# Output projection of a graph attention layer: chunk pairs per block, sums listed at the end of a step, another block order in the second pass

## The chip, the cores and the metric

The kernel runs on one core of a Trainium2 chip. The metric is the device time of one execution in microseconds; of several runs the median is taken. One further execution is recorded by the hardware profiler, and all the rows below come from it.

## What is computed

384 nodes with 1024 features go through one attention layer with an edge mask, in fp32:

```python
h = relu(layernorm(x))                                   # 384 x 1024
q, k, v = h @ wq.T + bq, h @ wk.T + bk, h @ wv.T + bv
q2, k2, v2 = q @ wiq.T + biq, k @ wik.T + bik, v @ wiv.T + biv   # each as 16 heads of 64
scores = einsum('hnd,hmd->hnm', q2, k2) / 8 + mask       # mask: softplus weight per edge type, -inf elsewhere
out = einsum('hnm,hmd->hnd', softmax(scores), v2)        # 384 x 1024
result = x + out @ wo.T + bo
```

The change is in the last line, out @ wo.T, and in how it is mixed with the heads.

## The kernel before

**Splitting.** Each fp32 product is made of three fp32r matmuls: high by high, high by low, low by high (mm3, L373 to L376). So every weight chunk (128 rows, 1024 columns) is split into a high and a low plane after it is loaded: the high one by ACT (L81) or VectorE (L79), the low one by VectorE or GpSimd (both L86). Loads are issued on SP's queue (L69), into four buffers.

**Phases.** First come the layer norm and the projections v, q, iv and k, while VectorE and GpSimd build the mask. Then one loop over steps (L825) does the attention and, in its gaps, what is left of the projections. This loop is where the change lies.

**The step loop.** Step i handles one tile i of the scores: head i // 3, row block i % 3, 48 tiles in all. What one tile passes through is spread over steps:
- S(i), step i: two score matmuls into one of two PSUM banks of tag "s" (L711).
- ttr(i), step i+1: VectorE adds the mask and takes the row's extreme, which reads that bank (L717).
- exp(i), step i+2: ACT (L721).
- recip(i), step i+3: VectorE (L734), and for i % 3 == 0 a scaling of it (L736); for the others GpSimd normalises the tile (L738).
- for i % 3 == 0: high(i) on ACT (L744, step i+3), low(i) on VectorE (L748, step i+4), and a transposing DMA on SP's queue (L752).
- the other two tiles of a head are transposed on TensorE (L758) some steps later, together with the matmuls of the attention by v2 (L773); a step with these is longer. ACT (L766) and VectorE (L767) take the transposed tiles from PSUM one step later, ACT (L793) and VectorE (L794) the head's output, and ACT (L798) and GpSimd (L799) split it into the planes of ao.

All of it is recorded in the order in which the Python code runs, and each engine works off its own list in that order. So where a line of code stands decides what is queued behind it.

**The filling.** In each step fill() is called before and after S(i) and gives TensorE some more matmuls from a generator. First fill_qk() gives the projections of q2 and k2 for the later heads; a finished projection is taken out by qk_done (L384, L385), which also issues the copies ks<-nat (L590). Then fill_o() gives the output projection.

**The output projection.** There are six output blocks a = 0 to 5 (a row block of 128 by 512 columns, list OT, L655) and eight chunks k of wo. Block (a,k) is three matmuls of 512 columns (omm, L650). Only three banks of tag "g" are free for sums, so there are two passes. The first takes chunks 0 to 3 (KH = 4) of each a; the sum is then added to the residual in SBUF by VectorE, ysum (L660 to L664), and the bank is free for another a. The second takes chunks 4 to 6 of a = 0 to 4, on three g banks and two s banks; the last part after the loop takes chunk 7, adds and stores. A block waits for its chunk's preparation (wready, two steps after it) and for the heads that it needs (6k + 18).

**When a ysum is listed.** A finished a is put on the list ysums. flush_y(1) inside fill_o() records one ysum just ahead of each bank("g") (L681, L697), that is, when a later a asks for the bank.

**When a chunk is prepared.** Chunks 0 and 1 are prepared while the q2 and k2 chunks are. Chunks 2 to 7 are prepared at the end of the steps listed in WSTEPS (L852), by wo_prep (L639): chunk 2 by VectorE (high) and GpSimd (low), 3, 4 and 6 by ACT and GpSimd, 5 and 7 by ACT and VectorE. wo_prep(k) also issues the load of chunk k+3, so that of chunk 2 issues the load of chunk 5.

Of the kernel before, what the change touches and what calls it, by code (L numbers as in the profile page):

```python
# [26 lines left out]
def gnn_kernel(ctx: ExitStack, tc: tile.TileContext, x, edges, erows, etw, wq, wk, wv, wiq, wik, wiv, wo,  # L27
# [20 lines left out]
    def bank(tag):  # L48
        return psum.tile([128, 512], F32, tag=tag, name=tag, bufs={"g": 3, "a": 1}.get(tag, 2))
# [545 lines left out]
    def run_tasks():  # L595
        while tasks:
            tasks.pop(0)()
# [31 lines left out]

    DT = (0,)  # L630
    PRE, RATE, RATE_O, RATE_E = 84, 7.9, 8, 8
    WSTEPS = (37, 40, 42, 44, 47, 51)
    PAR, OPOOL, ODVE = 1, (2, 3, 4, 6), (2,)

    otile = {}
# [1 line left out]
    KH = 4  # L637

    def wo_prep(k):  # L639

        dst = None
        if k == 4:
            otile[0] = gtile("g3").rearrange("p a k n -> p (a k n)")
        if 4 <= k < 7:
            g, b = otile[0], (k - 4) * 2048
            dst = (g[:, b:b + 1024], g[:, b + 1024:b + 2048])
        split(WO + k, nc.gpsimd if k in OPOOL else None, dst, k in ODVE)
        load(WO + k + 3)

    def omm(t, h, k, c=(0, 512)):  # L650
        hi, lo = (a[:, h * 512 + c[0]:h * 512 + c[1]] for a in whl[WO + k])
        mm3(oacc[t, h][:, c[0]:c[1]], ao[:, 0, k, t * 128:(t + 1) * 128], ao[:, 1, k, t * 128:(t + 1) * 128],
            hi, lo, k in (0, KH), k in (KH - 1, KT - 1))
# [6 lines left out]
    def ysum(a, c=(0, 512)):  # L660
        t, h = OT[a]
        y = xb[t][:, h * 512 + c[0]:h * 512 + c[1]]
        nc.vector.tensor_tensor(y, oacc[t, h][:, c[0]:c[1]], y, OP.add)  # L663
        return y  # L664
# [3 lines left out]
    def flush_y(n=6):  # L668
        for _ in range(min(n, len(ysums))):
            ysum(ysums.pop(0))  # L670

    def fill_o():


        first = [(0, 0), (0, 1), (1, 0), (1, 1), (2, 0), (2, 1)]
        first += [(a, k) for k in (2, 3) for a in range(3)] + [(a, k) for a in range(3, 6) for k in range(KH)]
        for a, k in first:
            while now[0] < wready[k] or now[0] < 6 * k + OREADY:
                yield 0
            if k == 0:  # L680
                flush_y(1)  # L681
                oacc[OT[a]] = bank("g")
            omm(*OT[a], k)
            if k == KH - 1:
                ysums.append(a)
            yield 4
        bank_step = (0, 0, 0, 49, 50)
        todo = [(a, k) for k in range(KH, 7) for a in range(5)]
        while todo:
            ready = [q for q in todo if now[0] >= max(6 * q[1] + OREADY, wready[q[1]], bank_step[q[0]])]  # L690
            if not ready:
                yield 0
                continue
            a, k = ready[0]
            todo.remove(ready[0])
            if k == KH:
                flush_y(1)  # L697
                oacc[OT[a]] = bank("gggss"[a])
            omm(*OT[a], k)
            yield 4  # L700
# [4 lines left out]
    def do_S(i):  # L705
        h, t = divmod(i, 3)
        p, o = divmod(h, 2)
        qs, ks = stacks["q", p], stacks["k", p]
        ps = st_ps[i] = bank("s")
        for s in range(2):  # L710
            nc.tensor.matmul(ps[:, :N], qs[:, o, t * 128:(t + 1) * 128], ks[:, o, s, :], start=(s == 0), stop=(s == 1))  # L711

    def do_ttr(i):
        t = i % 3
        e = es[i] = work.tile([128, N], F32, tag="e", name="e", bufs=EB)
        s = sts[i] = work.tile([128, 4], F32, tag="s", name="s", bufs=12)
        nc.vector.tensor_tensor_reduce(e, st_ps.pop(i)[:, :N], ma[:, t, :], -0.125, 3.0e38, OP.add, OP.min, s[:, 0:1])  # L717

    def do_exp(i):
        s = sts[i]  # L720
        nc.scalar.activation(es[i], es[i], AF.Exp, bias=s[:, 0:1], scale=-1.0, accum_out=s[:, 1:2])  # L721
# [10 lines left out]
    def do_norm(i):  # L732
        s = sts[i]
        nc.vector.reciprocal(s[:, 2:3], s[:, 1:2])  # L734
        if i % 3 in DT:
            nc.vector.tensor_scalar(s[:, 2:3], s[:, 2:3], PSC, None, op0=OP.mult)  # L736
        else:
            nc.gpsimd.tensor_tensor(es[i], es[i], s[:, 2:3].to_broadcast([128, N]), OP.mult)  # L738
# [3 lines left out]
    def do_high(i):  # L742
        planes[i] = plv[i // 3 % 3]
        nc.scalar.activation(planes[i][:, 0, :], es[i], AF.Copy, scale=sts[i][:, 2:3])  # L744

    def do_low(i):
        pl = planes[i]
        nc.vector.scalar_tensor_tensor(pl[:, 1, :], es.pop(i), sts[i][:, 2:3], pl[:, 0, :], op0=OP.mult, op1=OP.subtract)  # L748

    def do_turn(i):  # L750
        h, t = divmod(i, 3)
        nc.sync.dma_start_transpose(ptv[h % 3][:, :, t * 128:(t + 1) * 128],  # L752
                                    planes.pop(i).rearrange("p a n -> p (a n)"))
# [7 lines left out]
    def do_pt(i):  # L761
        h, t = divmod(i, 3)
        pt = ptv[h % 3]
        hi, lo = (pt[:, s * 3:s * 3 + 3, t * 128:(t + 1) * 128] for s in range(2))
        pv = tps.pop(i)[:, :N].rearrange("p (k n) -> p k n", k=3)
        nc.scalar.activation(hi, pv, AF.Copy, scale=PSC)  # L766
        nc.vector.scalar_tensor_tensor(lo, pv, PSC, hi, op0=OP.mult, op1=OP.subtract)  # L767
# [9 lines left out]
    def turns_and_av(tiles, heads):  # L777
        a, b = ([g(x) for x in xs] for g, xs in ((turn_mm, tiles), (av_mm, heads)))
        a, b = (itertools.chain(*x) for x in (a, b))
        end = object()  # L780
        while True:
            x, y = next(a, end), next(b, end)
            if x is end and y is end:
                return

    def do_ao(h):
        p, o = divmod(h, 2)
        if o == 0:
            aof[p] = work.tile([128, N], F32, tag="aof", name="aof")
        tmp = work.tile([128, N], F32, tag="aot", name="aot", bufs=1)  # L790
        ps = avs.pop(h)
        m, l = slice(o * 64, o * 64 + 64), slice(64 - o * 64, 128 - o * 64)
        nc.scalar.activation(tmp[m, :], ps[l, :N], AF.Identity, scale=down[l], bias=bc[m, 40 + p:41 + p])  # L793
        nc.vector.scalar_tensor_tensor(aof[p][m, :], ps[m, :N], down[m], tmp[m, :], op0=OP.mult, op1=OP.add)  # L794

    def do_aos(h):
        p = h // 2
        nc.scalar.activation(ao[:, 0, p, :], aof[p], AF.Copy)  # L798
        nc.gpsimd.tensor_tensor(ao[:, 1, p, :], aof[p], ao[:, 0, p, :].bitcast(F32), OP.subtract)  # L799

    gens = [fill_qk(), fill_o()]
    credit = [0.0]

    def fill(n):
        credit[0] += n
        while credit[0] > 0 and gens:
            try:
                c = next(gens[0])
            except StopIteration:
                gens.pop(0)  # L810
                continue
            if c == 0:
                credit[0] = 0.0
                return
            credit[0] -= c
# [9 lines left out]
    for i in range(S + 11):  # L825
        now[0] = i
        r = RATE if len(gens) == 2 else RATE_O if i < S else RATE_E
        fill(r / 2)
        if i < S:
            do_S(i)  # L830
        fill(r / 2)
        if 0 <= i - 1 < S:
            do_ttr(i - 1)
        if 0 <= i - 4 < S and (i - 4) % 3 in DT:
            do_low(i - 4)
        if 0 <= i - 2 < S:
            do_exp(i - 2)
        if 0 <= i - 3 < S:
            do_norm(i - 3)
            if (i - 3) % 3 in DT:  # L840
                do_high(i - 3)
        turns_and_av(t_at.get(i, []), [a_at[i]] if i in a_at else [])
        for x in t_at.get(i - 1, []):
            do_pt(x)
        if i - 1 in a_at:
            do_ao(a_at[i - 1])
        if a_at.get(i - 2, 0) % 2:
            do_aos(a_at[i - 2])
        run_tasks()
        if 0 <= i - 4 < S and (i - 4) % 3 in DT:  # L850
            do_turn(i - 4)
        if i in WSTEPS:  # L852
            wo_prep(wp)
            wready[wp] = i + 2
            wp += 1
    while gens:
        now[0] = 999
        fill(999)
# [55 lines left out]
```

## Time and profile before

| | us |
|---|---|
| median of 3 runs | 296.02 |
| the runs | 296.02, 294.78, 296.08 |
| the profiled execution | 294.56 |
| its span, from the first instruction to the last | 292.8 |
| TensorE busy in the span | 284.7 |
| VectorE busy | 208.2 |
| ACT busy | 159.7 |
| GpSimd busy | 154.8 |

The engines are called PE (TensorE), PEld (its weight loads), DVE (VectorE), ACT, POOL (GpSimd) and SP (the engine that issues DMAs) in the rows. A row of the timeline gives the start and the duration in us, the engine, the line of code, the operation, output<-inputs with their shapes, and in brackets how long the engine stood idle before it and what released it. Several like instructions in a row are merged (x2), with the time of all. A table by stages gives for each stretch the busy time of PE, PEld, DVE, ACT and POOL with the number of instructions, the granted clock of TensorE, the mean share of the DMA engines and what they moved in GB/s. A row of the waits names the engine and the instruction that waited, then the one waited for, the us in total, how often, and the longest. The chain of waits is followed back from the last instruction; "issue" in it is time for which the profile shows no wait.

### The profile page before, as it was taken

The numbers are of one execution on the slowest core, as the hardware profiler recorded it, in microseconds if no ns is written. First come the engines' busy times: TensorE is split into PE (matmuls) and PEld (weight loads), VectorE is DVE, ScalarE is ACT, GpSimd is POOL, SyncE is SP. The second block draws the span as 40 slices with busy tenths as digits, with TensorE's granted clock in tenths as the row PEclk, the third lists the DMA queues.
The fourth block names the chain that finished last, engine by engine and source line by source line (L and its number), as shares of the span: only waits on it lengthen the run. The fifth ranks groups of instructions, "written<-read, shape, count | busy, mean of one in ns | idle before, by whom it ended". The sixth has DMA issues, their size and how long they took to land. (4 is left out here: it accounts for less than half of the span.)

```text
span 292.8 us, 4859 instructions
## 1 busy us (share of the span) xinstructions
PE 284.7 (97%) x1610; PEld 267.4 (91%) x1610; DVE 208.2 (71%) x509; ACT 159.7 (55%) x291; POOL 154.8 (53%) x153
## 2 busy tenths in 40 slices
PE   6999999999999999999999999999999999989995
PEld 5999999999988889999999999999999998868874
DVE  3858996667665452999966768878786876788623
ACT  3894543244331222343643778787878788766510
POOL 3765576437775787992004256262627268636210
PEclk9999999999999999999999999999999999999999
DMA  7799857973463342278438879879797969901105
GB/s 268 248 321 404 292 209 254 323 242 112 143 189 122 121 146 72 72 224 296 154 86 227 241 208 211 212 166 227 166 234 147 254 133 234 230 2 27 27 3 215
DMA packets 33305, 54.60 MB, mean 187 GB/s; under 512 B 17408, under 2 KB 20992, under 8 KB 33280
## 3 DMA queue, kind: packets, MB, share of 16 engines
q1 hardware_dynamic: 30896, 51.90, 61.4%
q0 software_dynamic: 2064, 1.80, 2.2%
q10 hardware_dynamic: 320, 0.59, 0.8%
q8 instruction: 13, 0.21, 0.3%
q14 instruction: 12, 0.10, 0.1%
HBM read 38.30 MB, written 3.39 MB: 142 GB/s over the span
## 5 line engine op out<-in xcount | busy, mean ns | idle before, releaser
L374 PE MATMUL g<-g,whl 128*128 128x384 f32 x312 | 105.8, 339 | 0.0
L376 PE MATMUL g<-g,whl 128*128 128x384 f32 x312 | 104.3, 334 | 0.0
L375 PE MATMUL g<-g,whl 128*128 128x384 f32 x312 | 104.2, 334 | 0.0
L231 POOL DMA_INDIRECT tab<-val,idx x51 | 59.7, 1171 | 32.0 <-issue 11.8
L81 ACT ACTIVATE whl<-raw 128x1024 fp32r<-128x1024 f32 x51 | 53.5, 1050 | 29.8 <-PE g L376 21.1
L86 DVE TENSOR_TENSOR whl<-raw,whl 128x1024 fp32r<-128x1024 f32 x41 | 53.8, 1313 | 20.1 <-ACT whl L81 17.0
L374 PEld LDWEIGHTS g<-g,whl 128*128 128x128 f32 x312 | 58.6, 188 | 0.2
L375 PEld LDWEIGHTS g<-g,whl 128*128 128x128 f32 x312 | 58.6, 188 | 0.0
L376 PEld LDWEIGHTS g<-g,whl 128*128 128x128 f32 x312 | 58.6, 188 | 0.1
L390 ACT ACTIVATE g<-f,bc 128x384 fp32r<-128x384 f32 x24 | 14.8, 618 | 53.7 <-DVE f L389 44.8
L738 POOL TENSOR_TENSOR e<-e,s 128x384 f32<-128x384 f32 x32 | 26.4, 829 | 31.2 <-DVE s L734 23.0
L86 POOL TENSOR_TENSOR whl<-raw,whl 128x1024 fp32r<-128x1024 f32 x11 | 26.3, 2395 | 25.9 <-ACT whl L81 25.0
L721 ACT ACTIVATE e<-e,s 128x384 f32<-128x384 f32 x48 | 29.1, 607 | 2.0 <-DVE s L717 1.2
L717 DVE CUSTOM_DVE_ANT_0 e<-s,ma 128x384 f32<-128x384 f32 x48 | 26.4, 552 | 4.3 <-PE s L711 3.7
L389 DVE TENSOR_TENSOR f<-g,rrow 128x384 f32<-128x384 f32 x24 | 13.3, 554 | 18.0 <-PE g L376 18.0
L773 PE MATMUL a<-pt,vhl 128*128 128x384 f16 x96 | 26.1, 326 | 0.0
L758 PE MATMUL t<-ident,e 128*128 128x128 f32 x96 | 24.9, 272 | 0.0
L711 PE MATMUL s<-ks,qs 128*128 128x384 f32 x96 | 24.5, 335 | 0.0
L767 DVE SCALAR_TENSOR_TENSOR pt<-t,pt 128x384 f16<-128x384 f32 x32 | 16.6, 549 | 8.2 <-ACT pt L766 8.2
L799 POOL TENSOR_TENSOR g<-aof,g 128x384 fp32r<-128x384 f32 x8 | 8.3, 1041 | 25.5 <-ACT g L798 25.5
L711 PEld LDWEIGHTS s<-ks,qs 128*128 128x128 f32 x96 | 17.5, 188 | 0.9
L744 ACT ACTIVATE pt<-e,s 128x384 f16<-128x384 f32 x16 | 9.9, 616 | 15.4 <-issue 9.4
(166 smaller groups left out, 447.0 us busy)
## 6 DMA issues: line engine op xcount, KB each, us to landing
ks<-nat SPq DMA_DIRECT2D x30, 192.0 KB
raw<-in_wv_dram SPq DMA_DIRECT2D x8, 512.0 KB
raw<-in_wq_dram SPq DMA_DIRECT2D x8, 512.0 KB
raw<-in_wiv_dram SPq DMA_DIRECT2D x8, 512.0 KB
raw<-in_wk_dram SPq DMA_DIRECT2D x8, 512.0 KB
raw<-in_wiq_dram SPq DMA_DIRECT2D x8, 512.0 KB
raw<-in_wik_dram SPq DMA_DIRECT2D x8, 512.0 KB
raw<-in_wo_dram SPq DMA_DIRECT2D x8, 512.0 KB
```

The lines of the kernel that those rows point to most:

```text
L81: nc.scalar.activation(dst[0], raw[w], AF.Copy)
L86: (eng or nc.vector).tensor_tensor(lo, raw[w], hi.bitcast(F32), OP.subtract)
L231: nc.gpsimd.indirect_dma_start(out=tabs[c // RNG], out_offset=bass.IndirectOffsetOnAxis(ap=idx[:, c:c + 1], axis=0), in_=val[:, c:c + 1], ...
L374: nc.tensor.matmul(ps, lhi, rhi, start=first, stop=False)
L375: nc.tensor.matmul(ps, lhi, rlo, start=False, stop=False)
L376: nc.tensor.matmul(ps, llo, rhi, start=False, stop=last)
L711: nc.tensor.matmul(ps[:, :N], qs[:, o, t * 128:(t + 1) * 128], ks[:, o, s, :], start=(s == 0), stop=(s == 1))
L717: nc.vector.tensor_tensor_reduce(e, st_ps.pop(i)[:, :N], ma[:, t, :], -0.125, 3.0e38, OP.add, OP.min, s[:, 0:1])
L721: nc.scalar.activation(es[i], es[i], AF.Exp, bias=s[:, 0:1], scale=-1.0, accum_out=s[:, 1:2])
L738: nc.gpsimd.tensor_tensor(es[i], es[i], s[:, 2:3].to_broadcast([128, N]), OP.mult)
L758: nc.tensor.transpose(ps[:, k * 128:(k + 1) * 128], es[i][:, k * 128:(k + 1) * 128], ident)
L773: nc.tensor.matmul(ps[:, :N], vhl[:, k, h, :, :], ptv[h % 3][:, 3 * s + k, :], start=(k == 0 and s == 0), stop=(k == 2 and s == 1))
```

## The change

```diff
-    WSTEPS = (37, 40, 42, 44, 47, 51)
+    WSTEPS = (36, 38, 42, 44, 47, 51)
...
-        first = [(0, 0), (0, 1), (1, 0), (1, 1), (2, 0), (2, 1)]
-        first += [(a, k) for k in (2, 3) for a in range(3)] + [(a, k) for a in range(3, 6) for k in range(KH)]
+        first = [(a, k) for c in (0, 2) for a in range(3) for k in (c, c + 1)]
+        first += [(a, k) for a in range(3, 6) for k in range(KH)]
...
             if k == 0:
-                flush_y(1)
                 oacc[OT[a]] = bank("g")
...
-        todo = [(a, k) for k in range(KH, 7) for a in range(5)]
+        todo = [(a, k) for k in range(KH, 7) for a in (0, 1, 3, 4, 2)]
...
             if k == KH:
-                flush_y(1)
                 oacc[OT[a]] = bank("gggss"[a])
...
             wo_prep(wp)
             wready[wp] = i + 2
             wp += 1
+        flush_y()
```

Chunk 2 is prepared at the end of step 36 instead of 37, chunk 3 at the end of step 38 instead of 40; with them the loads of chunks 5 and 6 are issued earlier. In the first pass a = 0, 1, 2 take chunks 0 and 1 each as before, and then chunks 2 and 3 as a pair per a, not chunk 2 of all three and then chunk 3. The ysums that have become due are all listed at the end of each step, behind the step's other work, and no longer ahead of the bank that they free. In the second pass a = 2 comes last within each chunk, so that both s banks are asked for before the third g bank.

By the code the step in which a block of the first pass, a ysum or a bank is recorded is this (a block that fill() gives ahead of S(i) is marked <):

| step | before | after |
|---|---|---|
| 40 | (2,1)<, (0,2) | (2,1)<, (0,2) |
| 41 | (1,2)<, (2,2) | (0,3)<, (1,2), ysum 0 |
| 42 | (0,3)<, (1,3) | (1,3)<, (2,2), ysum 1 |
| 43 | (2,3)<, ysum 0, bank 3, (3,0) | (2,3)<, bank 3, (3,0), ysum 2 |
| 44 | (3,1)<, (3,2) | (3,1)<, (3,2) |
| 45 | (3,3)<, ysum 1, bank 4, (4,0) | (3,3)<, bank 4, (4,0), ysum 3 |
| 46 | (4,1)<, (4,2) | (4,1)<, (4,2) |
| 47 | (4,3)<, ysum 2, bank 5, (5,0) | (4,3)<, bank 5, (5,0), ysum 4 |
| 48 | (5,1), (5,2) | (5,1), (5,2) |
| 49 | (5,3), ysum 3, bank 0, (0,4) | (5,3), bank 0, (0,4), ysum 5 |
| 50 | ysum 4, bank 1, (1,4), ysum 5, bank 2, (2,4) | bank 1, (1,4), bank 3, (3,4) |
| 51 | bank 3, (3,4), bank 4, (4,4) | bank 4, (4,4), bank 2, (2,4) |

## The prediction

> **What bounds the kernel now.** I read the page first: the share of each engine.
>
> ```profile
> PE 284.7 (97%) x1610; PEld 267.4 (91%) x1610; DVE 208.2 (71%) x509; ACT 159.7 (55%) x291; POOL 154.8 (53%) x153
> ```
>
> TensorE works nearly the whole span, so an order that keeps its instructions can only win where it stands still. Second, the table by stages of 5 us over the end, where the change lies, and TensorE's waits after 225 us:
>
> ```profile
> 255.00:260.00 5.00, 3.88 (x22) 3.06 (x19) 3.46 (x5) 3.31 (x6) 2.36 (x3) 1.00 0.13 26
> 260.00:265.00 5.00, 4.75 (x26) 4.03 (x27) 3.83 (x15) 3.23 (x9) 2.61 (x3) 1.00 0.21 43
> PE g L374 <- DVE res L663: 1.4, 1, 1.4
> ```
>
> There is one hole: 1.12 us in one row and 0.25 in the next, 1.37 together, and one wait of 1.4 us, a matmul for a ysum (L663). The clock column is 1.00, so the throttle has no part. Third, the timeline shows which step it is, by the score matmuls, one pair per step:
>
> ```profile
> 256.62 0.52 PE L711 MATMUL s<-ks,qs 128*128 128x384 f32 x2
> 258.37 0.51 PE L711 MATMUL s<-ks,qs 128*128 128x384 f32 x2
> 260.25 0.50 PE L374 MATMUL g<-whl,g 128*128 128x512 f32 x1 [1.37 <-DVE res L663]
> 261.76 0.51 PE L711 MATMUL s<-ks,qs 128*128 128x384 f32 x2
> ```
>
> Counted back from S(47), the last pair, these are S(44), S(45), S(46). A step with two blocks and no transposes takes 258.37 - 256.62 = 1.75 us; S(45) to S(46) is such a step and takes 3.39. So **1.64 us** are lost, a little more than the idle time, since the pipeline fills again. Fourth, the chain that ended last, around this hole:
>
> ```profile
> 257.17 1.07 ACT g L81
> 258.30 1.20 issue
> 259.51 0.70 DVE res L663
> 260.25 0.50 PE g L374
> ```
>
> The wait is for ysum(1), which frees the bank that a=4 needs. It stands late because VectorE was told it only when that bank was asked for, in step 45, behind the preparation of wo chunk 5: ACT's high part (L81), then VectorE's low part (L86, called "issue" here; its row is below).
>
> **Part 1: the pairs and the ysums at the end of a step (saves 1.64).** Following the code, a=0 now ends in step 41, a=1 in 42, a=2 and 3 in 43 and 45, so ysum(1) is told at the end of step 42 and not in 45. Every block and its three matmuls remain. These are VectorE, ACT and GpSimd before, steps 41 to 45:
>
> ```profile
> 250.33 0.61 DVE L794 SCALAR_TENSOR_TENSOR aof<-a,vsc,aot 64x384 f32<-64x384 f32 x1
> 251.52 0.15 DVE L736 TENSOR_SCALAR s<-s 128x1 f32<-128x1 f32 x1
> 251.71 0.69 DVE L663 TENSOR_TENSOR res<-g,res 128x512 f32<-128x512 f32 x1
> 252.32 0.55 DVE L717 CUSTOM_DVE_ANT_0 e<-s,ma 128x384 f32<-128x384 f32 x1
> 253.80 0.56 DVE L717 CUSTOM_DVE_ANT_0 e<-s,ma 128x384 f32<-128x384 f32 x1 [0.32 <-PE s L711]
> 255.67 0.56 DVE L767 SCALAR_TENSOR_TENSOR pt<-t,pt 128x384 f16<-128x384 f32 x1 [1.23 <-ACT pt L766]
> 258.27 1.23 DVE L86 TENSOR_TENSOR g<-raw,g 128x1024 fp32r<-128x1024 f32 x1 [0.46 <-ACT g L81]
> 251.76 0.62 ACT L744 ACTIVATE pt<-e,s 128x384 f16<-128x384 f32 x1 [0.73 <-ACT e L721]
> 252.28 1.04 ACT L81 ACTIVATE g<-raw 128x1024 fp32r<-128x1024 f32 x1
> 253.40 2.38 POOL L86 TENSOR_TENSOR g<-raw,g 128x1024 fp32r<-128x1024 f32 x1 [2.21 <-ACT g L81]
> ```
>
> A ysum holds VectorE 0.61 us (251.71 to the 252.32 of the next). New order: ysum(0) at 250.9 behind L794, so L736(39) ends at 252.35 and not 251.67; then ysum(1) to 253.0, ttr(42) to 253.5, low(39) to 254.1, ysum(2) to 254.9, ttr(43) to 255.4. The two idle times before (0.32 and 1.23) take up what was added: L767 keeps its 255.67. Each ysum's matmuls are over when it is told (block (1,3) by 251.5, the start of S(42) in its step), so VectorE waits for none. Banks 3, 4 and 5 are asked for in steps 43, 45 and 47, each after its ysum's end.
>
> What is late next? S(46) writes the bank that ttr(44) reads. ttr(44) stands behind L86 at 259.51, in the place that ysum(1) had, and ends at 260.06; with the 0.05 us that TensorE took in the hole (259.51 + 0.69 to 260.25) S(46) can start at 260.11. It is due at 258.37 + 1.75 = 260.12. So the new bound just meets the old one: I take 0 lost here, the bounds being 0 and 0.83, one L738 of GpSimd in the way (below).
>
> **Part 2: chunks 2 and 3 prepared in steps 36 and 38 instead of 37 and 40 (I take 0).** The instructions stay, four on the engines and two loads, but three queues change.
>
> ```profile
> 238.68 0.56 DVE L717 CUSTOM_DVE_ANT_0 e<-s,ma 128x384 f32<-128x384 f32 x1
> 241.23 0.69 DVE L79 CAST whl<-raw 128x1024 fp32r<-128x1024 f32 x1
> 244.12 0.56 DVE L717 CUSTOM_DVE_ANT_0 e<-s,ma 128x384 f32<-128x384 f32 x1
> 242.05 2.42 POOL L86 TENSOR_TENSOR whl<-raw,whl 128x1024 fp32r<-128x1024 f32 x1 [0.94 <-PE t L758]
> 246.39 0.51 PE L711 MATMUL s<-ks,qs 128*128 128x384 f32 x2
> ```
>
> The cast goes to 238.68, ahead of ttr(36), and GpSimd's low part follows its end by some 0.13 (241.92 to 242.05 before): 239.5 to 241.9. It stands there ahead of L738(34). VectorE's low(33) is ready at about 239.85, inside it. What that does is shown by one place of the trace:
>
> ```profile
> 266.82 2.40 POOL L86 TENSOR_TENSOR g<-raw,g 128x1024 fp32r<-128x1024 f32 x1 [2.08 <-ACT g L81]
> 267.88 1.75 DVE L748 SCALAR_TENSOR_TENSOR pt<-e,s,pt 128x384 f16<-128x384 f32 x1 [0.24 <-ACT pt L744]
> L748 DVE SCALAR_TENSOR_TENSOR pt<-e,s,pt x16: 611/619/1754, 166.6 to 267.9; 128x384 f16<-128x384 f32 x16
> ```
>
> The one low() of 16 that started inside a GpSimd L86 took 1.75 us and ended 0.41 after it. So low(33) would end at 242.3, two us late. Queued behind it: recip(34), L385 of the last ik chunk (to 243.0), ttr(37) (243.5), two L767 and L794 (245.2), ttr(38) at 245.8. ttr(38) releases S(40), due at 246.39: 0.6 us of cover are left, and without it each further us is a us of TensorE. low(36) then meets chunk 3's low part (244.6 to 247.0), and the lag is gone by the L767 of step 41. L738(34) and (35) end by 244.6, ahead of the transposes of step 40, which come after S(40). On ACT L81 of chunk 3 now stands ahead of exp(37), 1 us, taken up by step 41. By the Trainium skill (SBUF — State Buffer, "Who interferes with whom") a VectorE instruction with two SBUF inputs fully blocks while a GpSimd instruction that reads SBUF runs; the row agrees (1.75 against 0.62), and by the rule low(33) pays as I have it, still under cover.
>
> SP's queue: the load of chunk 5 moves ahead of the four ks copies of the last head pair.
>
> ```profile
> 239.04 0.59 SPq L69 DMA_DIRECT2D raw<-in_wo_dram  x1
> 239.68 1.24 SPq L752 DMA_TRANSPOSE pt<-pt  x1
> 241.35 2.80 SPq L590 DMA_DIRECT2D ks<-nat  x4
> ks<-nat SPq DMA_DIRECT2D x30, 192.0 KB
> raw<-in_wo_dram SPq DMA_DIRECT2D x8, 512.0 KB
> 241.00:247.00 6.00, 6.00 (x34) 5.16 (x32) 5.03 (x17) 4.58 (x12) 4.18 (x4) 1.00 1.07 241
> 254.00:257.00 3.00, 3.00 (x20) 2.56 (x20) 1.51 (x5) 2.02 (x5) 3.00 (x3) 1.00 0.34 68
> 251.51 0.51 PE L711 MATMUL s<-ks,qs 128*128 128x384 f32 x2
> ```
>
> The copies wait for L385 and are issued from 243.1 to 245.9. Loads 4 and 5 and the copies are 2 x 512 + 4 x 192 KB = 1.8 MB, at the 241 GB/s of that stretch 7.6 us from 239.04: 246.7; with a transpose between, and the issue's end at 245.9, I put the landing at 248 to 249. S(42), the first that needs them, is due at 251.51.
>
> **Part 3: the second pass in another order (0).** Before, ysum(4) and (5) were told together, next to their banks:
>
> ```profile
> 269.63 1.26 DVE L663 TENSOR_TENSOR res<-g,res 128x512 f32<-128x512 f32 x2
> 271.26 0.40 PE L374 MATMUL g<-g,g 128*128 128x512 f32 x1
> ```
>
> They ended at 270.89, 0.37 before the matmul of a=2. With TensorE 1.6 us earlier that would fail; but a=3 and 4 (on s banks, free once ttr(46) and (47) are done, by 266.4) now go first, a=2 starts three blocks after a=1, at about 271, and ysum(5), told at the end of step 49, ends at about 269.2. So the gain is kept. From there to the end the order of the last blocks and the output is as before: TensorE, its last ysum and the store move up together.
>
> **Sum.** 294.56 - 1.64 + 0 = 292.9 for the profiled execution (its span 292.8, 1.8 around it). The three runs shown have the median 296.02; the profiled one lies below all three, 1.46 under the median. Nothing in the change bears on that difference, so for the median I take the same step: 296.02 - 1.64 = **294.4**.
>
> **Rivals.**
> *GpSimd takes the gain (within 0.5%).* In part 1 low(39) starts at L736's end + 0.61 + 0.55 = about 253.5, chunk 4's low part when ACT has done L744 and L81, about 253.95. If GpSimd is first by a slip of over 0.45 us, low(39) ends at 253.95 + 2.38 + 0.41 = 256.7; then ysum(2), ttr(43), two L767, L794, L86 and ttr(44) follow, 261.4, and S(46) starts 1.35 late: 1.64 - 1.35 = 0.3 saved, 295.7. The order of starts speaks against it, the 1.75 us row for it. The Trainium skill's rule above speaks for it too.
> *The wait moves to S(46).* If L738(41) of GpSimd (to about 258.2) is still running when VectorE's L86 comes at 258.27, that is up to 0.83 late, and so is S(46): 0.8 saved, 295.2.
> *The ks copies come late (slower).* For it: the DMA share of 1.07, a full queue. Against: the bytes above. If they land only when the stretch's transfers die away, at about 254.2 (68 GB/s from 254 on), S(42) stands still for 2.7 us: 2.7 - 1.64 = 1.1 slower, 297.1. It costs from a landing at 251.5 and is slower than before from 253.1.
> *The change does nothing*, because the bank was free anyway: the wait's row and the chain name ysum(1), so I give it almost nothing.
>
> **How the numbers follow.** Forecast 0.62, GpSimd 0.13, S(46) 0.11, ks copies 0.13, nothing 0.01. A measurement of this kernel tells about 0.5%, 1.48 us, from no change; the forecast's 1.64 lies barely beyond it, with runs 1.3 us apart, so of its 0.62 I count 0.47 as faster and 0.15 as same. The range goes from 292.9 (the sum on the profiled execution) up to 296.0, beyond GpSimd's 295.7; it leaves out the ks case and some of the forecast.
>
> **What would show it.** Right: no wait of TensorE for L663, S(45) to S(46) 1.75 us, a ysum between L736 and ttr(42), a low() of about 2.4 us near 240, and S(40) and S(42) unmoved. Wrong: TensorE waiting for L717 at S(40) or S(46), for a DMA at S(42), or an L748 of 2 us or more after 253.

## The result, and the profile after

| | before | after |
|---|---|---|
| median, us (22 runs each) | 294.64 | 293.17 |
| lowest to highest run | 294.28 to 296.25 | 292.80 to 294.72 |
| ratio to before, 95% interval | | 0.995 (0.9937 to 0.9963) |
| profiled execution's span | 292.8 | 291.4 |

The change saves 1.47 us, 0.5%, with an interval of 0.37% to 0.63%. The runs of both kernels lie in two groups some 1.4 us apart (before: 294.3 to 295.0, and 295.9 to 296.3; what parts them is left open); two of the three runs known ahead of the prediction were of the upper group, hence their median of 296.02.

First the engines' line of the page, then the table by stages (PE, PEld, DVE, ACT, POOL busy, clock, DMA share, GB/s), then the waits of TensorE after 225 us, all of the changed kernel. Below its line 690 the lines are two lower than before: S is L709, ttr L715, L732 recip, L734 its scaling, L736 GpSimd's normalising, high L742, low L746.

```profile
PE 284.9 (98%) x1610; PEld 267.5 (92%) x1610; DVE 208.8 (72%) x509; ACT 159.8 (55%) x291; POOL 152.5 (52%) x153
```

```profile
255.00:260.00 5.00, 5.00 (x28) 4.25 (x26) 3.52 (x8) 3.53 (x8) 3.06 (x3) 1.00 0.20 39
260.00:265.00 5.00, 5.00 (x28) 4.09 (x27) 4.48 (x16) 4.41 (x10) 2.84 (x3) 1.00 0.22 43
```

```profile
PEld s L709 <- DVE s L715: 0.3, 1, 0.3
PEld g L376 <- POOL g L797: 0.3, 1, 0.3
PEld L771 <- issue: 0.3, 1, 0.3
```

The hole is gone: both stretches are full, and no wait for L663 is left. What remains are three waits of weight loads (PEld), 0.3 us each. Two of them the kernel before has as well; the first is new, S(46) for ttr(44). In the timeline of TensorE, S(44) to S(46), the first matmul behind them, and S(47); then S(47) of the kernel before:

```profile
256.72 0.52 PE L709 MATMUL s<-ks,qs 128*128 128x384 f32 x2
258.48 0.51 PE L709 MATMUL s<-ks,qs 128*128 128x384 f32 x2
260.25 0.61 PE L709 MATMUL s<-ks,qs 128*128 128x384 f32 x2
260.69 0.40 PE L374 MATMUL g<-whl,g 128*128 128x512 f32 x1
...
263.72 0.52 PE L709 MATMUL s<-ks,qs 128*128 128x384 f32 x2
```

```profile
265.13 0.52 PE L711 MATMUL s<-ks,qs 128*128 128x384 f32 x2
```

S(45) to S(46) is 1.77 us, from 3.39; the normal step is 1.76 (256.72 to 258.48). S(46) takes 0.10 more than its neighbour, and the block behind it starts 0.44 after it where the step before needs some 0.36. From S(44) to S(47) TensorE takes 7.00 us, from 8.51 (256.62 to 265.13): 1.51 saved, so of the 1.64 us some 0.1 stayed.

VectorE in steps 41 to 45, and GpSimd's low part of chunk 4:

```profile
250.96 0.67 DVE L663 TENSOR_TENSOR res<-g,res 128x512 f32<-128x512 f32 x1
252.22 0.15 DVE L734 TENSOR_SCALAR s<-s 128x1 f32<-128x1 f32 x1
252.29 0.68 DVE L663 TENSOR_TENSOR res<-g,res 128x512 f32<-128x512 f32 x1
253.36 0.62 DVE L746 SCALAR_TENSOR_TENSOR pt<-e,s,pt 128x384 f16<-128x384 f32 x1
253.96 0.68 DVE L663 TENSOR_TENSOR res<-g,res 128x512 f32<-128x512 f32 x1
255.78 0.56 DVE L765 SCALAR_TENSOR_TENSOR pt<-t,pt 128x384 f16<-128x384 f32 x1 [0.59 <-ACT pt L764]
258.37 1.22 DVE L86 TENSOR_TENSOR g<-raw,g 128x1024 fp32r<-128x1024 f32 x1 [0.46 <-ACT g L81]
259.62 0.56 DVE L715 CUSTOM_DVE_ANT_0 e<-s,ma 128x384 f32<-128x384 f32 x1
```

```profile
254.10 2.38 POOL L86 TENSOR_TENSOR g<-raw,g 128x1024 fp32r<-128x1024 f32 x1 [4.08 <-ACT g L81]
```

Three ysums stand where there was one. low(39) starts at 253.36, 0.74 us ahead of GpSimd's L86, and is not held. VectorE's lag is gone by 255.78, with 0.59 us of idle time in front of that instruction. Behind L86, ttr(44) now follows at once.

Steps 36 to 40 on VectorE, GpSimd and TensorE (S(40)):

```profile
238.73 0.68 DVE L79 CAST whl<-raw 128x1024 fp32r<-128x1024 f32 x1
239.81 2.55 DVE L746 SCALAR_TENSOR_TENSOR pt<-e,s,pt 128x384 f16<-128x384 f32 x1
245.09 0.56 DVE L715 CUSTOM_DVE_ANT_0 e<-s,ma 128x384 f32<-128x384 f32 x1
```

```profile
239.55 2.38 POOL L86 TENSOR_TENSOR whl<-raw,whl 128x1024 fp32r<-128x1024 f32 x1 [0.91 <-issue]
```

```profile
246.50 0.51 PE L709 MATMUL s<-ks,qs 128*128 128x384 f32 x2
```

low(33) takes 2.55 us, from 0.62: it ends 0.43 us after GpSimd's L86. ttr(38) ends at 245.65, and S(40) comes at its time, with 0.85 us left.

SP's queue (load of chunk 5, then the ks copies) and S(42):

```profile
241.11 0.52 SPq L69 DMA_DIRECT2D raw<-in_wo_dram  x1
242.97 3.14 SPq L590 DMA_DIRECT2D ks<-nat  x4
```

```profile
251.62 0.51 PE L709 MATMUL s<-ks,qs 128*128 128x384 f32 x2
```

S(42) isn't late. How long the four ks copies took from the start of their issue to their landing, in the same trace:

```profile
DMA to landing us min/median/max: 4.7/4.8/4.9
```

The last of them is issued at 244.8, so they had landed by about 249.7, some 1.9 us ahead of S(42). In the second pass, ysum(5) and the first block of a=2:

```profile
268.22 0.67 DVE L663 TENSOR_TENSOR res<-g,res 128x512 f32<-128x512 f32 x1
```

```profile
271.23 0.39 PE L374 MATMUL g<-g,g 128*128 128x512 f32 x1
```

The sum is ready 2.3 us ahead, where before it was 0.37.

### The profile page after: what moved, and what is told of

Same layout as the page of the kernel before. It is cut to its first block, busy times and chain, and to the rows that moved or that the text cites. A ratio compares the mean times of both kernels' runs of the same rounds, so it can differ in the third digit from the quotient of the medians.

```text
span 291.4 us, 4858 instructions
## 1 busy us (share of the span) xinstructions
PE 284.9 (98%) x1610; PEld 267.5 (92%) x1610; DVE 208.8 (72%) x509; ACT 159.8 (55%) x291; POOL 152.5 (52%) x153
## 3 DMA queue, kind: packets, MB, share of 16 engines
HBM read 38.30 MB, written 3.39 MB: 143 GB/s over the span
## 4 chain that ended last, share of the span: by engine, by line
PE 95%; DMA 2%; DVE 1%; SPq 0%; issue 0%
PE g L376 22%; PE g L374 22%; PE g L375 22%; PE s L709 6%; PE a L771 5%; PE t L756 4%; DMA g<-in_x_dram 2%; PE s L374 2%; PE s L376 2%; PE s L375 2%; PE g L423 2%; PE t L376 2%; PE t L375 2%; PE t L374 2%; PE a L374 1%; PE a L376 1%
## 5 line engine op out<-in xcount | busy, mean ns | idle before, releaser
L231 POOL DMA_INDIRECT tab<-val,idx x51 | 57.1, 1120 | 34.8 <-issue 10.2
L81 ACT ACTIVATE whl<-raw 128x1024 fp32r<-128x1024 f32 x51 | 53.6, 1050 | 29.4 <-PE g L376 21.1
L86 DVE TENSOR_TENSOR whl<-raw,whl 128x1024 fp32r<-128x1024 f32 x41 | 53.5, 1306 | 20.0 <-ACT whl L81 20.0
L736 POOL TENSOR_TENSOR e<-e,s 128x384 f32<-128x384 f32 x32 | 26.3, 826 | 30.6 <-DVE s L732 21.5
L86 POOL TENSOR_TENSOR whl<-raw,whl 128x1024 fp32r<-128x1024 f32 x11 | 26.3, 2395 | 25.8 <-ACT whl L81 21.2
L715 DVE CUSTOM_DVE_ANT_0 e<-s,ma 128x384 f32<-128x384 f32 x48 | 26.4, 552 | 3.7 <-PE s L709 3.1
L709 PE MATMUL s<-ks,qs 128*128 128x384 f32 x96 | 24.6, 336 | 0.0
L797 POOL TENSOR_TENSOR g<-aof,g 128x384 fp32r<-128x384 f32 x8 | 8.7, 1091 | 23.9 <-ACT g L796 23.9
L742 ACT ACTIVATE pt<-e,s 128x384 f16<-128x384 f32 x16 | 9.9, 616 | 15.7 <-issue 9.1
L709 PEld LDWEIGHTS s<-ks,qs 128*128 128x128 f32 x96 | 17.4, 188 | 1.1 <-DVE s L715 0.3
```

The lines of the kernel that those rows point to most:

```text
L81: nc.scalar.activation(dst[0], raw[w], AF.Copy)
L86: (eng or nc.vector).tensor_tensor(lo, raw[w], hi.bitcast(F32), OP.subtract)
L231: nc.gpsimd.indirect_dma_start(out=tabs[c // RNG], out_offset=bass.IndirectOffsetOnAxis(ap=idx[:, c:c + 1], axis=0), in_=val[:, c:c + 1], ...
```

## The experiments

My theory: the whole gain is the one wait of bank 4 for ysum(1), which VectorE had queued behind its L86 of chunk 5; pairs, earlier preparation and the second order save nothing by themselves. The rivals: one of those parts gives the gain; or VectorE's meetings with GpSimd cost or save TensorE time. The results first, each against runs of the kernel before on the same chip. The intervals of the kernels that save something overlap, so which of them saves more is read from their traces:

| kernel | median, us | before, us | ratio, 95% interval |
|---|---|---|---|
| before + listing at the end of a step | 293.76 | 294.72 | 0.996 (0.994 to 0.9981) |
| before + second order | 294.85 | 294.72 | 1.0009 (0.9987 to 1.003) |
| before + earlier preparation | 294.62 | 294.72 | 0.9997 (0.9975 to 1.0018) |
| before + chunk 5's low part on GpSimd | 293.03 | 294.72 | 0.9956 (0.9935 to 0.9978) |
| before + pairs + earlier preparation | 294.70 | 294.64 | 1.0008 (0.9985 to 1.0031) |
| before + listing, chunk 4 in step 43 | 293.41 | 294.64 | 0.9965 (0.9942 to 0.9989) |
| after, chunk 2's low part on VectorE | 293.15 | 294.64 | 0.9947 (0.9926 to 0.9968) |
| after + 6 reductions in step 37 | 296.72 | 294.64 | 1.0052 (1.0026 to 1.0077) |
| after + 1 reduction | 293.13 | 294.62 | 0.9942 (0.9916 to 0.9969) |
| after + 3 reductions | 294.14 | 294.62 | 0.9983 (0.9961 to 1.0004) |
| after + chunk 5's low part on GpSimd | 292.96 | 294.62 | 0.9951 (0.9931 to 0.9971) |
| before + chunk 5 on GpSimd, last low plane on VectorE | 292.68 | 294.62 | 0.9941 (0.9919 to 0.9963) |

### Each part alone

**Second order alone.**

```diff
-        todo = [(a, k) for k in range(KH, 7) for a in range(5)]
+        todo = [(a, k) for k in range(KH, 7) for a in (0, 1, 3, 4, 2)]
```

> The kernel before, with the second pass's order 0, 1, 3, 4, 2 and nothing else. My theory: 0 (within 0.2 us), the wait of 1.4 us for ysum(1) stays. The rival that the order of the banks at the end gives the gain: about 1.5 us saved.

No gain; the wait of 1.4 us is there as before.

**Earlier preparation alone.**

```diff
-    WSTEPS = (37, 40, 42, 44, 47, 51)
+    WSTEPS = (36, 38, 42, 44, 47, 51)
```

> The kernel before, with chunks 2 and 3 prepared in steps 36 and 38 and nothing else. My theory: 0 (within 0.2 us): low(33) takes about 2.5 us behind GpSimd, S(40) isn't late, the wait of 1.4 us for ysum(1) stays. The rival that earlier preparation gives the gain: 1 us or more saved; the rival that GpSimd's block costs TensorE time: slower.

Neither gain nor loss. TensorE's wait and low(33) in this kernel (low is L748 here):

```profile
PE g L374 <- DVE res L663: 1.4, 1, 1.4
```

```profile
239.79 2.54 DVE L748 SCALAR_TENSOR_TENSOR pt<-e,s,pt 128x384 f16<-128x384 f32 x1
```

**Pairs and earlier preparation, without the listing.** The pairs need chunk 3 in time, so they can't be tried without the other.

```diff
+    WSTEPS = (36, 38, 42, 44, 47, 51)
...
+        first = [(a, k) for c in (0, 2) for a in range(3) for k in (c, c + 1)]
+        first += [(a, k) for a in range(3, 6) for k in range(KH)]
```

> The change without the listing at the end of a step and without the second order: pairs, and chunks 2 and 3 in steps 36 and 38, with each ysum still told where its bank is asked for. My theory: ysum(1) stays in step 45 behind chunk 5's L86, so the wait of 1.4 us stays and nothing is saved (within 0.2 us). The rival that the pairs give the gain because a sum is finished earlier: 1 us or more saved.

No gain either: a sum that is ready two steps earlier helps nobody while its ysum is listed in step 45. TensorE's wait is the same row as in the last kernel, 1.4 us for L663.

**The listing alone.**

```diff
             if k == 0:
-                flush_y(1)
                 oacc[OT[a]] = bank("g")
...
             if k == KH:
-                flush_y(1)
                 oacc[OT[a]] = bank("gggss"[a])
...
             wo_prep(wp)
             wready[wp] = i + 2
             wp += 1
+        flush_y()
```

> The kernel before, with the ysums listed at the end of each step and nothing else of the change. My theory (the gain is the wait for ysum(1) behind chunk 5's L86): that wait goes, since ysum(1) is told in step 42. But ysum(0) and ysum(1) now both stand between L736(39) and low(39): low(39) comes at about 253.5, GpSimd's low part of chunk 4 starts at 253.4. If GpSimd is first, low(39) takes over 2 us and S(46) starts some 0.7 us late: 0.9 us saved, ratio 0.997. If low(39) is first: 1.6 us saved, 0.9945. The rival that pairs or earlier preparation give the gain: 0 saved.

0.96 us saved, near the 0.9 of the first case; the interval (0.6 to 1.8 us) holds the 1.6 of the second as well, and the trace decides for the first. VectorE (ysum(1), low(39)), GpSimd (chunk 4) and S(46) of this kernel:

```profile
252.81 0.69 DVE L663 TENSOR_TENSOR res<-g,res 128x512 f32<-128x512 f32 x1 [0.36 <-PE g L376]
253.89 2.35 DVE L746 SCALAR_TENSOR_TENSOR pt<-e,s,pt 128x384 f16<-128x384 f32 x1
```

```profile
253.45 2.38 POOL L86 TENSOR_TENSOR g<-raw,g 128x1024 fp32r<-128x1024 f32 x1 [2.21 <-ACT g L81]
```

```profile
260.94 0.61 PE L709 MATMUL s<-ks,qs 128*128 128x384 f32 x2 [0.61 <-DVE s L715]
```

The wait for L663 is gone, but both ysums fall in step 42, and in the old order block (1,3) stands behind S(42), so that VectorE waits 0.36 us for it. low(39) comes 0.44 us after GpSimd's start and is held for 2.35 us. All that follows is late, and S(46) stands still for 0.61 us. This is my rival "GpSimd takes the gain", at a little over half of its price: S(46) comes 0.76 late, not 1.35. So this is what the pairs do, with the earlier preparation that they need: they spread the ysums over steps 41 and 42. With ysum(0) in step 41, low(39) starts at 253.36 and not 253.89; and since high(39) on ACT waits for the L734 behind that ysum, and the L81 of chunk 4 stands behind high(39), GpSimd starts at 254.10 and not 253.45. The order of the two turns round.

**The listing, with chunk 4 a step later.** The control for the last kernel: the same two ysums, but GpSimd's L86 behind low(39). The diff is against that kernel.

```diff
-    WSTEPS = (37, 40, 42, 44, 47, 51)
+    WSTEPS = (37, 40, 43, 44, 47, 51)
```

> The kernel before with the listing at the end of a step, and chunk 4 prepared in step 43 instead of 42, so that low(39) starts ahead of GpSimd's L86 of chunk 4 with two ysums before it. My theory: low(39) takes 0.62 us, no wait for L663, about 1.5 us saved (0.995). Against the same without the later chunk 4 this tells what the meeting of low(39) and GpSimd costs.

1.23 us saved, a little less than expected. VectorE (low(39), L86 of chunk 5), GpSimd (the L736 behind chunk 4) and S(45) and S(46):

```profile
254.27 0.61 DVE L746 SCALAR_TENSOR_TENSOR pt<-e,s,pt 128x384 f16<-128x384 f32 x1
...
258.69 1.46 DVE L86 TENSOR_TENSOR g<-raw,g 128x1024 fp32r<-128x1024 f32 x1 [0.46 <-ACT g L81]
```

```profile
258.25 0.83 POOL L736 TENSOR_TENSOR e<-e,s 128x384 f32<-128x384 f32 x1
```

```profile
258.80 0.51 PE L709 MATMUL s<-ks,qs 128*128 128x384 f32 x2
260.81 0.61 PE L709 MATMUL s<-ks,qs 128*128 128x384 f32 x2
```

low(39) is back at 0.61 us. But now VectorE's L86 (raw and high plane, both in SBUF) meets GpSimd's L736 and takes 1.46 instead of 1.23, and S(46) comes 0.26 late (2.01 instead of 1.75): the other rival, "the wait moves to S(46)", in small.

### The cause alone

**Chunk 5's low part on GpSimd, nothing of the change.**

```diff
-    PAR, OPOOL, ODVE = 1, (2, 3, 4, 6), (2,)
+    PAR, OPOOL, ODVE = 1, (2, 3, 4, 5, 6), (2,)
```

> The kernel before, with the low part of chunk 5 made by GpSimd and not VectorE, and nothing of the change. It takes L86 away from in front of ysum(1). My theory: ysum(1) starts at about 257.8, TensorE doesn't wait for it, 1.6 us saved, as much as the whole change (0.995); low(42) stands about 1.8 us behind GpSimd, under cover. If the wait had another cause than what stands ahead of ysum(1): 0.

One number gives 1.69 us, as much as the whole change. ysum(1) and low(42) on VectorE, and S(45) and S(46):

```profile
257.66 0.69 DVE L663 TENSOR_TENSOR res<-g,res 128x512 f32<-128x512 f32 x1
...
259.82 1.14 DVE L748 SCALAR_TENSOR_TENSOR pt<-e,s,pt 128x384 f16<-128x384 f32 x1 [0.20 <-ACT pt L744]
```

```profile
258.20 0.51 PE L711 MATMUL s<-ks,qs 128*128 128x384 f32 x2
259.92 0.51 PE L711 MATMUL s<-ks,qs 128*128 128x384 f32 x2
```

ysum(1) is listed in step 45 as before, only with nothing slow ahead of it, and TensorE doesn't wait for it. So the wait needs both, the late listing and L86 ahead of it in VectorE's queue: taking away either one ends it.

**The same on top of the change.** The diff is the same.

> The changed kernel with the low part of chunk 5 on GpSimd. My theory: the wait for ysum(1) is gone already, so the two don't add up: only the rest of S(46)'s wait, 0.1 us, goes, ratio to before 0.9945 to 0.995. A rival by which the change and L86 are two separate costs: another 1.5 us saved, 0.990.

292.96 us, 0.2 less than the changed kernel's 293.17, which these intervals don't tell from nothing. The two are two ways to the same gain, and don't add up. S(45) and S(46) now keep the normal step:

```profile
258.36 0.51 PE L709 MATMUL s<-ks,qs 128*128 128x384 f32 x2
260.10 0.51 PE L709 MATMUL s<-ks,qs 128*128 128x384 f32 x2
```

### VectorE's lag and its cover

**Chunk 2's low part on VectorE**, in the changed kernel.

```diff
-    PAR, OPOOL, ODVE = 1, (2, 3, 4, 6), (2,)
+    PAR, OPOOL, ODVE = 1, (3, 4, 6), (2,)
```

> The changed kernel, with the low part of chunk 2 made by VectorE and not GpSimd. My theory: low(33) falls from 2.55 us to 0.62, VectorE works 1.23 us more, S(40) isn't late either way, so the time stays that of the changed kernel (ratio to before 0.995, within 0.001). If the two us of low(33) had cost TensorE anything, this would be faster than the changed kernel.

293.15 us: the same. low(33) in this kernel:

```profile
242.48 0.61 DVE L746 SCALAR_TENSOR_TENSOR pt<-e,s,pt 128x384 f16<-128x384 f32 x1
```

It isn't held, but VectorE has chunk 2's L86 (1.23 us) to do instead. ttr(38) ends at 246.39, 1.52 us ahead of S(40) at 247.91, where the changed kernel has 0.85. These 0.67 us less of lag bought nothing: the lag of the changed kernel was under cover.

**More work on VectorE in step 37**, in the changed kernel, six reductions:

```diff
         run_tasks()
+        if i == 37:
+            for _ in range(6):
+                nc.vector.tensor_reduce(vmax[:, 6:7], ma[:, 0, :], axis=AX.X, op=OP.max)
```

> The changed kernel with six more VectorE reductions (384 elements, result not used) at the end of step 37, some 0.5 us each, 2.8 us in all. My theory: ttr(38) ends at about 248.4 and S(40), due at 246.5, waits for it: TensorE stands still there for about 2 us, and the kernel is slower than the one before by about 0.5 us. If S(40) has more cover than I think, less is lost.

Slower by 2.08 us than before in the median, not by 0.5. The twelve runs fall apart by the mean granted clock: five have 0.999 or 1.000 and take 295.62 to 295.95 us, seven have 0.994 and take 296.68 to 298.65. The profiled execution is the slowest of the seven. Its reductions, S(39) and the first matmuls behind it, and the clock a little later (the number ahead of the last two in the last row, 0.50):

```profile
244.67 3.48 DVE L850 TENSOR_REDUCE vmax<-ma 128x1 f32<-128x384 f32 x6
```

```profile
248.68 0.67 PE L709 MATMUL s<-ks,qs 128*128 128x384 f32 x2 [1.96 <-DVE s L715]
249.14 0.63 PE L374 MATMUL g<-whl,g 128*128 128x512 f32 x1
249.57 0.63 PE L375 MATMUL g<-whl,g 128*128 128x512 f32 x1
```

```profile
250.00:251.00 1.00, 1.00 (x4) 0.81 (x3) 0.93 (x5) 0.00 (x0) 1.00 (x2) 0.50 1.12 145
```

The expectation failed in three places. The reductions took 3.48 us, not 2.8. ttr(37) stands behind them as well, and so S(39) stood still first, for 1.96 us: in the changed kernel ttr(37) ends at 243.41, 1.35 us ahead of S(39) at 244.76, and 2.8 us would have used that up too. And in this execution the granted clock then fell to 0.50, and the matmuls came 0.43 apart and not 0.23. The cover of 0.85 us at S(40) was right: 3.48 less 0.85 is 2.63, and the five runs at the full clock have a median of 295.67, 2.50 us above the changed kernel. The four fastest of the other seven (296.68 to 296.83) are some 1.1 us above those five.

**One reduction**, 0.54 us.

> The changed kernel with one more VectorE reduction at the end of step 37, 0.57 us. My theory: S(40) has 0.85 us of cover in the changed kernel (ttr(38) ends at 245.65, due at 246.5), so this costs nothing: the time of the changed kernel, ratio to before 0.995, and no wait of S(39) or S(40). If VectorE's lag there reached TensorE at once: 0.5 us slower than the changed kernel.

293.13 us, the time of the changed kernel, and no wait at S(39) or S(40): under cover.

**Three reductions**, 1.71 us.

> The changed kernel with three more reductions at the end of step 37, 1.7 us. My theory: S(39) is late by about 0.4 us and S(40) by another 0.45, so 0.9 us more than the changed kernel, 0.6 us less than before (0.998). The granted clock stays at 1.00, since no hole is longer than the 1.4 us of the kernel before; if it falls all the same, 1 us or more is added.

294.14 us, 1.0 more than the changed kernel. S(39) and S(40) of this kernel:

```profile
245.24 0.61 PE L709 MATMUL s<-ks,qs 128*128 128x384 f32 x2 [0.18 <-DVE s L715]
247.49 0.62 PE L709 MATMUL s<-ks,qs 128*128 128x384 f32 x2 [0.26 <-DVE s L715]
```

S(39) is 0.34 late against the normal step (S(38) at 243.15), near 1.71 less its cover of 1.35; S(40) is 0.50 later still, and the clock in these stretches is 1.00. With 0.54 us of extra work neither is late; with 1.71 us S(40) is 0.84 late in all, that is 1.71 less the cover of 0.85: cover, then one for one.

### A better version

```diff
-    PAR, OPOOL, ODVE = 1, (2, 3, 4, 6), (2,)
+    PAR, OPOOL, ODVE = 1, (2, 3, 4, 5, 6), (2,)
...
-        nc.gpsimd.tensor_tensor(ao[:, 1, p, :], aof[p], ao[:, 0, p, :].bitcast(F32), OP.subtract)
+        (nc.vector if p == 7 else nc.gpsimd).tensor_tensor(ao[:, 1, p, :], aof[p], ao[:, 0, p, :].bitcast(F32), OP.subtract)
```

> The kernel before with the low part of chunk 5 on GpSimd, and the low plane of the last two heads of ao made by VectorE, which is idle there, and not by GpSimd; nothing of the change. My theory: as with chunk 5 alone 1.6 to 1.7 us saved, and TensorE's 0.3 us wait for GpSimd's L799 at the first block of chunk 7 goes, worth about 0.1: ratio 0.994 to 0.995.

292.68 us, 0.9941 of before (0.9919 to 0.9963), the lowest median of all. The first block of chunk 7 runs without its pause, its third matmul and the next block 0.23 apart:

```profile
281.49 0.39 PE L376 MATMUL g<-whl,g 128*128 128x512 f32 x1
281.72 0.39 PE L374 MATMUL g<-whl,g 128*128 128x512 f32 x1
```

After 200 us TensorE waits in this kernel for one weight load of 0.3 us only. Whether it beats the changed kernel's 293.17 can't be told by these intervals alone; that the waits for ttr(44) and for GpSimd's split of ao are gone is seen in its trace.

## Why the prediction was right

- **The bound.** One loss of 1.64 us, ysum(1) behind chunk 5's L86: shown by taking L86 away alone (1.69 us saved) and by the listing alone (the wait goes). Right.
- **Part 1, the sum.** 1.64 was forecast, 1.47 measured (0.37% to 0.63%, or 1.1 to 1.9 us). The interval is 0.13% to either side, so a saving of this size stood out more clearly than the 0.5% that I took for what can be told. Of the mechanism of this part nothing failed; the term mis-sized is S(46), for which I took 0 between bounds of 0 and 0.83. The step S(45) to S(46) takes 0.02 us more than 1.75, and the next, S(46) to S(47), 3.47 where the kernel before takes 3.37: 0.12 in all. With chunk 5's L86 on GpSimd it goes (1.74 for the step).
- **The order of low(39) and GpSimd.** Forecast 253.5 against 253.95, measured 253.36 against 254.10. By the prediction's own rows GpSimd's start comes to 254.08 (253.40 and the 0.68 by which L736 moves), so the margin was 0.57 and not 0.45. Right in the changed kernel; the listing alone shows the rival as a fact, low(39) 0.44 us too late and 0.76 us lost at S(46) (260.94 against 258.43 + 1.75).
- **Part 2.** low(33) was to end at 242.3 and ttr(38) at 245.8; they ended at 242.36 and 245.65, and cost nothing (earlier preparation alone, and chunk 2 on VectorE). The cover was 0.85 us, not 0.6. That beyond it each further us is a us of TensorE holds for 1.7 us of extra work, and for 3.5 in the runs at the full clock; where the clock fell, some 1.1 us came on top.
- **The ks copies.** S(42) wasn't late. The copies landed at about 249.7, some 0.7 us behind the forecast's 248 to 249 and well ahead of 251.6; that a landing after that would cost was not tried.
- **Part 3.** The second order saves nothing alone, as forecast. I argued that without it the gain would fail at bank 2, since ysum(4) and (5) were listed together. But in the changed kernel ysum(5) is ready at 268.9, 2.3 us before its bank is used, and the listing alone, in the old order, has no wait for L663. So this step of the argument failed: nothing here shows a need for the second order. The changed kernel without it was not run.
- **The absolute time.** 294.4 was forecast and 293.17 measured. The step that failed is the one by which I carried the saving over to the median of three runs, 296.02; over 22 runs the median before is 294.64, and the profiled execution's 294.56 was the better base: 294.56 - 1.64 = 292.9. The range held because its lower end was worked out on that base; that the forecast itself lies 1.2 us too high is the price of the other.

## What to carry to other kernels

To mend a wait, look at the queue of the engine that is waited for: what counts is not only when an instruction's inputs are ready but what is listed ahead of it, and one slow instruction moved to an idle engine can do as much as a new order. Before an instruction is moved on VectorE, look which of GpSimd's long ones it will meet: 0.44 us in the wrong order cost low(39) 1.7 us here, and TensorE 0.76 of the 1.64 us. And write the cover next to each lag: 0.85 us at S(40) held for 0.54 and failed for 1.71.

## What the runs showed of the hardware

- **VectorE held by GpSimd.** Each low() that started inside a GpSimd L86 ended 0.40 to 0.43 us after it, in every trace (2.55, 2.35 and 1.75 us instead of 0.62, for example); the ysums (0.67 to 0.69 us) and ttr (0.54 to 0.56), which take one input from PSUM, took no longer beside an L86. It goes the other way as well: GpSimd's split of ao (L797) takes 1.01 us alone and up to 1.34 where it starts while a low() runs, and the less of the low() is left, the less it grows (1.27 with 0.40 us left, 1.03 with 0.16).
- **After a hole of 1.96 us the clock was halved, in some executions.** With six reductions the granted clock of the profiled execution was 0.50 from about 249 to 252 us, after 1.96 us without a matmul. Seven of that kernel's twelve runs show the lower mean clock, 0.994, and five don't, with the same code; only the one execution was traced. So the clock can halve after such a hole and need not. In the profiled executions holes of 1.37 us (before) and of 0.61 (listing alone) left it at 1.00. By the Trainium skill (TensorE: Matmul & The Clock Gate, "Part 1: The HAM clock gate") the array falls to half its clock after an idle window of about 3.4 us. The half agrees; here less than 2 us of standing still were enough, and about 3 us of half clock followed.
